# An unread full-array product in the empty places of attention's first steps

## The chip, the cores and the metric

The kernel runs on one NeuronCore of a Trainium2 chip. The metric is the device time of one execution in microseconds (us). Engine names are those of the profile: PE is TensorE's matmul, PEld its weight load, DVE is VectorE, ACT is ScalarE, POOL is GpSimd, SP is SyncE, which issues most DMAs. "Granted clock" (PEclk) is the share of TensorE's full clock that the throttle let through.

## What is computed

Two layers on 8 sequences of 512 tokens with 256 features, all in float32. Layer 0 is a bidirectional state-space mixer beside a mixture of eight experts that picks one expert per token. Layer 1 is attention with 16 heads of 16 features beside a mixture of seven experts (and a no-op), two per token, with a capacity per expert. Only layer 1 matters here:

```python
x = x + attention0(xn) + experts0(xn)
xn = layernorm(x)
scores = clip(q @ k.T * scale, -10000, 10000) * decay      # 16 heads, 512 x 512
scores = clip(scores)                                     # per batch
attn = softmax(scores); out = attn @ v                    # latent keys and values
x = x + out @ Wo + experts1(xn)                           # top 2 of 8, capacity 512 rows each
```

## The kernel before, in words

The program is one hand-ordered stream (each engine runs its instructions in the order in which the Python code issues them; a semaphore wait holds back everything behind it on the same engine). After the state-space layer comes attention, which is 128 **steps**: 8 batches, 4 groups of 4 heads, 4 tiles of 128 query rows. The loop `for n in range(N + 3)` (L1612) issues in each turn, in this order on PE:

- `scores` of step n (L1463): four products of 16x128 by 16x512, side by side in the array, each into one of the four `s_ps` banks. DVE then clips them (L1468) and multiplies by the decay band with a running maximum (L1470), four each; ACT takes the exponentials (L1478) one turn later.
- in even turns, `values` (L1494) of the two steps before: 16 products with 256 columns into `o_ps`.
- a place for other work, `fill()` (L1568).
- `transpose` (L1485) of heads 0 and 1 of step n-2: eight 128x128 transposes into the two `p_ps` banks, copied out by ACT (L1486).
- a second place, then the transposes of heads 2 and 3, then a third and a fourth place. So a turn of this part of the program has four places.

What goes into a place is decided by `fill()`: first a piece already begun (`half_done`), then `urgent` (the closing projections of a batch, `finish`, L1426), then `idle`, which is the second layer's experts, paced by `due()`. While the layer before still has rows to finish (`late_left`), it does one piece of those (`last_rows`). Otherwise the place stays empty and `fill()` returns false.

The experts can't begin at once. First the routing must be worked out (`route1`, L1189: some 50 DVE instructions, two products L201 and L202 and one exponential, issued by `follow()` at the end of each turn, two pieces a turn). Then `send_rows` (L1333) sends 32 tiles of 128 rows to their slots, two tiles a turn: per tile, one DVE copy of slots (L1365), one DVE product (L1353) and two indirect DMAs by POOL (L1346). The turn in which these run out is `ready`; it is n = 23. The expert pieces are offered from n = `ready` + 3 = 26 on (L1634). So in turns 5 to 25 the four places are empty, except for turn 23, where `finish` of batch 0 takes all four.

All filled-in work shares one PSUM buffer: `bank(name, shape)` (L1183) takes a tile with the tag `bank` and one buffer, so a product in it must wait until whoever read the bank's former content has done so. The expert pieces are each four matmul instructions of 128x128 by 256 columns (L1279 for the first matrix, L1292 for the second). A float32 product is two matmul instructions in the trace. `ident` is the 128x128 identity, and `band` the decay table, 128 x 896, both constants by that time.

Of the kernel before, what the change touches and what calls it, by code (L numbers as in the profile page):

```python
# [17 lines left out]
P = 128  # L18
B, S, DM = 8, 512, 256
# [40 lines left out]
def tile_kernel(ctx: ExitStack, tc: tile.TileContext, t, out: bass.AP):  # L60
    nc = tc.nc
    V, A, G, T, Y = nc.vector, nc.scalar, nc.gpsimd, nc.tensor, nc.sync
# [4 lines left out]
    def ctile(name, shape, dtype=FP, pool=None):  # L67
        return (pool or const).tile(shape, dtype, name=name, tag=name)
# [7 lines left out]
    ident = ctile("ident", [P, P])  # L76
# [281 lines left out]
    def bank(name, shape, tag="gen"):  # L358
        return mp.tile(shape, FP, name=name, tag=("e", "s")[tag] if isinstance(tag, int) else tag, bufs=2)
# [150 lines left out]
    with ExitStack() as es:  # L510
# [560 lines left out]
        with tc.manual_schedule(engines=ENGINES):  # L1071
# [34 lines left out]
            def fill(n):  # L1106
                for _ in range(n):
                    if next(rows, "end") == "end":
                        next(rest, None)

            for n in range(N):
# [16 lines left out]
                if n % 8 == 5 and next_:  # L1128
                    pending.append(beginning)
                fill(1)  # L1130
                if ahead:
                    ahead.cross(range(NH // 2))
                now.inside()
                if ahead:
                    ahead.cross(range(NH // 2, NH))
                turn()
                fill(1)
                now.before()
                if ahead:
                    ahead.pairs(batch[ahead.b])  # L1140
                fill(1)
                turn()
                now.behind()
# [35 lines left out]
    with tc.tile_pool(name="a1", bufs=1) as p1, tc.tile_pool(name="a2", bufs=2) as p2, tc.tile_pool(  # L1179
# [153 lines left out]
        def send_rows():  # L1333

            sent = []
            for i in range(NTILE):
                b, c = i // TPB, i % TPB
                if c == 0 and b + 2 < B:
                    ask_rows(b + 2)
                if c == 0:  # L1340
                    V.tensor_copy(to_send[b][:, :, DM : DM + NE], to_send["shares"][:, i : i + TPB, :])
                    V.tensor_copy(to_send[b][:, :, DM + NE :], bc(iota_n[:, i : i + TPB], 2, [P, TPB, NE]))
                x = to_send[b][:, c, :]
                at = turn(r1b, i)
                for k in range(2):
                    one = G.indirect_dma_start(  # L1346
                        out=xd1, out_offset=bass.IndirectOffsetOnAxis(ap=at[:, k : k + 1], axis=0),
                        in_=x, in_offset=None, bounds_check=NSLOT1 - 1, oob_is_err=False,
                    )
                    for other in sent:  # L1350
                        tc.declare_no_dep(one.ins, other.ins, reason="rows go to slots of their own")
                    sent.append(one)
                V.tensor_scalar(x_sb[:, i, :], x[:, :DM], noop[:, i : i + 1], None, ALU.mult)  # L1353
                yield
# [79 lines left out]
        def combine():  # L1434


            def add(b):
                G.dma_start(out=x_sb[:, b * TPB : (b + 1) * TPB, :], in_=rows_of(x1, b), accum_op=ALU.add)

            for b in (B - 1, *range(B - 2)):  # L1440
                add(b)
            yield
            while B - 2 not in finished:
                yield
            add(B - 2)
            for b in range(B - 1):
                G.dma_start(out=rows_of(out, b), in_=x_sb[:, b * TPB : (b + 1) * TPB, :])
# [92 lines left out]
        with tc.manual_schedule(engines=ENGINES):  # L1540
# [11 lines left out]
            def due():  # L1552

                return WORK * (n - ready - 2) / (LAST - ready - 2)

            rows, routing, sends, work, ready, e1 = combine(), route1(), send_rows(), None, None, None
# [4 lines left out]
            def last_rows(k):  # L1561

                nonlocal late_left
                for _ in range(k):
                    if next(rest, "end") == "end":
                        late_left = False

            def fill():  # L1568

                nonlocal spent  # L1570
                while queue := half_done or urgent or (idle if idle and spent < due() else []):
                    try:
                        spent += queue[0] is work
                        if next(queue[0]):
                            half_done[:] = queue[:1]
                        else:
                            half_done.clear()
                        return True
                    except StopIteration:
                        queue.pop(0)  # L1580
                if late_left:
                    last_rows(1)
                return late_left

            def more():
# [177 lines left out]
```

## Time and profile before

| | |
|---|---|
| median of 9 runs | 2038.75 us (2034.35 to 2045.25) |
| the profiled execution | 2037.76 us, of which its span (first to last instruction) is 2036.1 us |
| mean granted clock in it | 0.941 |
| PE busy | 1823.4 us, 90% of the span |
| DVE busy | 1450.4 us, 71% |
| ACT busy | 1150.8 us, 57% |
| POOL busy | 628.3 us, 31% |
| attention's first scores | 1132.60 us from the span's start |
| scores of turn 5 / 9 / 23 / 24 / 26 / 27 begin | 1183.10 / 1221.94 / 1307.68 / 1315.96 / 1326.88 / 1336.42 us |
| granted clock from 1342.5 to 1980 us | 1.00 |

A view of stretches ("windows") gives, for each stretch of the span, how long each engine was busy in it, with the number of instructions in brackets, and then PEclk, the DMA engines' share and GB/s. A timeline row gives the start, the time, the engine, the line, the operation, what is written and read, how many were merged into the row (x8), and in brackets the engine's idle time before it and what ended that. Matmuls are pipelined: the time of one contains its way through the array, so what a group of them costs PE is read from the start of the next group, not from the sum of durations.

### The profile page before, as it was taken

Reading aid. Unit: us, or ns where it says so; the run is one execution under the profiler, and the core shown is the slowest. Engines: PE = TensorE matmul, PEld = TensorE weight load, DVE = VectorE, ACT = ScalarE, POOL = GpSimd, SP = SyncE. Lnnn points to the kernel's source line nnn. Section 1 sums busy time; section 2 is a strip of 40 time slices with the busy share of each in tenths; the row PEclk is TensorE's granted clock in tenths of the full one; section 3 lists DMA queues with packets and bytes.
Section 4 is the critical chain, followed back from the end, with each engine's and each line's share of the span. In section 5 each row is a group of like instructions: output and inputs, shape, how many; then the busy total and the mean of one; then the engine's idle time right before and its main releaser. Section 6 shows DMA issues by size and latency. Waiting matters only on the chain.

```text
span 2036.1 us, 33675 instructions
## 1 busy us (share of the span) xinstructions
PE 1823.4 (90%) x11760; PEld 1226.4 (60%) x11760; DVE 1450.4 (71%) x3431; ACT 1150.8 (57%) x2511; POOL 628.3 (31%) x570
## 2 busy tenths in 40 slices
PE   5676899999999999998799578899999999999997
PEld 4433577676767777764455344566666666666654
DVE  5775666667576665769743579978787878787785
ACT  1143353535445353544443258778887887788876
POOL 0038644646355454634341006500000100000030
PEclk9876999999999999998798678899999999999998
DMA  7112565655556565634443334223132222313180
GB/s 268 62 42 97 194 215 165 215 169 189 169 156 218 175 199 177 197 110 140 150 161 111 110 100 147 67 69 96 44 99 52 75 78 56 100 35 105 35 166 11
DMA packets 152025, 255.68 MB, mean 126 GB/s; under 512 B 22537, under 2 KB 111484, under 8 KB 139952
## 3 DMA queue, kind: packets, MB, share of 16 engines
q1 hardware_dynamic: 113872, 132.94, 21.2%
q0 software_dynamic: 28512, 110.92, 17.8%
q10 hardware_dynamic: 9472, 9.67, 1.4%
q8 instruction: 94, 1.54, 0.3%
q14 instruction: 75, 0.61, 0.1%
HBM read 185.38 MB, written 73.07 MB: 127 GB/s over the span
## 4 chain that ended last, share of the span: by engine, by line
PE 64%; DVE 11%; ACT 9%; issue 2%; DMA 2%; POOL 1%; SPq 1%; ACTq 0%; DVEq 0%; POOLq 0%
PE p_ps L1485 8%; PE o_ps L1494 6%; PE h_ps L564 6%; PE y_ps L582 6%; PE pj L772 6%; PE s_ps L1463 5%; ACT s L1478 5%; PE e_yp L1292 5%; PE e_hp L1279 5%; ACT pT L1486 3%; PE op L914 2%; PE yd L994 2%; PE seg L956 2%; PE sp L1020 2%; PE yoff L1012 1%
## 5 line engine op out<-in xcount | busy, mean ns | idle before, releaser
L1468 DVE TENSOR_SCALAR s<-s_ps 128x512 f32<-128x512 f32 x512 | 317.8, 682 | 142.7 <-PE s_ps L1463 138.2
L1478 ACT ACTIVATE s<-s,ng 128x512 f32<-128x512 f32 x512 | 330.7, 716 | 0.0
L1486 ACT COPY pT<-p_ps 128x512 f32<-128x512 f32 x512 | 276.0, 588 | 86.5 <-PE p_ps L1485 79.9
L1470 DVE CUSTOM_DVE_ANT_0 s<-s,band 128x512 f32<-128x512 f32 x512 | 323.1, 685 | 0.0
L1485 PE MATMUL p_ps<-ident,s 128*128 128x128 f32 x2048 | 288.3, 284 | 29.5 <-ACT pT L1486 23.8
L1485 PEld LDWEIGHTS p_ps<-ident,s 128*128 128x128 f32 x2048 | 235.5, 144 | 112.1 <-ACT s L1478 41.0
L1298 POOL DMA_INDIRECT x<-e_yo,e_to x28 | 45.8, 1636 | 588.5 <-ACT e_yo L1297 351.9
L772 PE MATMUL pj<-xT,w_in 128*128 128x512 f32 x384 | 203.7, 657 | 12.6 <-DVE cv L785 7.8
L1463 PE MATMUL s_ps<-kT,qT 16*128 16x512 f32 x1024 | 169.3, 682 | 29.9 <-DVE s L1468 22.8
L564 PEld LDWEIGHTS h_ps<-xdT,w 128*128 128x128 f32 x1248 | 149.4, 193 | 22.6 <-issue 21.5
L564 PE MATMUL h_ps<-xdT,w 128*128 128x128 f32 x1248 | 153.0, 276 | 3.1 <-DMA w<-in_w_dram,w_idx 3.1
L785 DVE SCALAR_TENSOR_TENSOR cv<-pj,w_conv_w,cv 128x511 f32<-128x511 f32 (+2 forms) x192 | 143.1, 746 | 11.1 <-ACT cv L781 7.1
L582 PE MATMUL y_ps<-w,hT 128*128 128x256 f32 x624 | 149.7, 384 | 0.0
L940 POOL TENSOR_TENSOR au<-da,half 128x512 f32<-128x512 f32 x64 | 77.7, 1214 | 226.3 <-PE seg L956 125.5
L1494 PE MATMUL o_ps<-pT,vt 128*32 128x256 f32 x2048 | 138.2, 413 | 0.1
L582 PEld LDWEIGHTS y_ps<-w,hT 128*128 128x128 f32 x624 | 117.4, 193 | 32.7 <-issue 17.4
L772 PEld LDWEIGHTS pj<-xT,w_in 128*128 128x128 f32 x384 | 71.9, 205 | 96.4 <-issue 85.6
L1279 PE MATMUL e_hp<-e_xdT,e_w 128*128 128x256 f32 x448 | 120.7, 392 | 7.6 <-ACT e_hT L1282 6.8
L1014 POOL TENSOR_TENSOR yT<-yT,ex 128x512 f32<-128x512 f32 (+1 forms) x48 | 58.6, 1220 | 223.2 <-DVE ex L1013 157.8
L1494 PEld LDWEIGHTS o_ps<-pT,vt 128*32 128x32 f32 x2048 | 64.2, 117 | 95.2 <-issue 65.6
L1292 PE MATMUL e_yp<-e_w,e_hT 128*128 128x256 f32 x448 | 113.1, 385 | 0.5 <-ACT e_hT L1282 0.5
L994 PE MATMUL yd<-mt,xdt 128*64 128x128 f32 x1024 | 77.4, 298 | 38.8 <-DVE mt L988 38.8
(289 smaller groups left out, 3015.1 us busy)
## 6 DMA issues: line engine op xcount, KB each, us to landing
ex<-exd SPq DMA_DIRECT2D x96, 128.0 KB
u<-in_u_dram SPq DMA_DIRECT2D x16, 512.0 KB
fr<-fdd SPq DMA_DIRECT2D x64, 128.0 KB
od<-os SPq DMA_DIRECT2D x28, 256.0 KB
e_w<-in_ei_dram SPq DMA_DIRECT2D x7, 1024.0 KB
e_w<-in_eo_dram SPq DMA_DIRECT2D x7, 1024.0 KB
xd<-xd SPq DMA_DIRECT2D x39, 128.0 KB
yd<-yo SPq DMA_DIRECT2D x39, 128.0 KB
```

The lines of the kernel that those rows point to most:

```text
L564: T.matmul(hp[:, i, :], w1[:, k * FF + f * P : k * FF + (f + 1) * P], xdT[:, k * P : (k + 1) * P], start=(k == 0), stop=(k == KC - 1),)
L582: T.matmul(yp, hT[f // 4][:, f % 4, :], w2[:, f * DM : (f + 1) * DM], start=(f == 0), stop=(f == FC - 1))
L772: T.matmul(pj, w_in[:, k, o * P : (o + 1) * P], self.xT[:, k, :], start=(k == 0), stop=(k == KC - 1))
L1279: T.matmul(hp, w1[:, k, f * P : (f + 1) * P], xdT[:, k, :], start=(k == 0), stop=(k == KC - 1))
L1292: T.matmul(yp, hT[:, f, c * P : (c + 1) * P], w2[:, f, :], start=(f == 0), stop=(f == FC - 1))
L1463: T.matmul(sp[i], self.q[r, cols], self.k[r, :], start=True, stop=True)
L1468: V.tensor_scalar(self.p[i], sp[i], -CLAMP, CLAMP, ALU.max, ALU.min)
L1470: V.tensor_tensor_reduce(out=self.p[i], in0=self.p[i], in1=band[:, at : at + S], scale=1.0, scalar=-3.0e38, op0=ALU.mult, op1=ALU.max, acc ...
L1478: A.activation(self.p[i], self.p[i], AF.Exp, bias=self.ng[:, i : i + 1])
L1485: T.transpose(pp[:, k, :], self.p[i][:, k * P : (k + 1) * P], ident)
L1486: A.copy(pT[i][:, :, cc * P : (cc + 1) * P], pp)
L1494: T.matmul(op[32 * i : 32 * i + 32, half * 2 * P : (half + 1) * 2 * P], self.v[:, k, h * (AD + 1) : h * (AD + 1) + 32], pT[i][:, k, :], st ...
```

## The change

Where `fill()` finds nothing, and the experts are not yet offered, it issues one product of the identity with the first 512 columns of the decay band, into the shared bank. Nobody reads it. `fill()` goes on returning `late_left`, which is false there, so what its callers do after it is as before.

```diff
@@ fill()
                 if late_left:
                     last_rows(1)
+                elif ready is None or n < ready + 3:
+                    T.matmul(bank("warm", [P, S]), ident, band[:, :S], start=True, stop=True)
                 return late_left
```

On PE the new order has 80 of these products (160 matmul instructions): four in each of turns 5 to 22, 24 and 25, none elsewhere. In a turn they stand after `scores` (and `values`), between the two pairs of transposes, and two behind the second pair. The order of the other engines' instructions and of all DMAs is as before.

## The prediction

> **What bounds the kernel now.** I read the page's slices first, to see where PE's clock drops; then the stretches of the turns concerned; then the timeline of PE inside a turn, to see what a filled place costs. The slices, each 50.9 us long (first rows of the page):
>
> ```profile
> PE   5676899999999999998799578899999999999997
> ...
> DVE  5775666667576665769743579978787878787785
> ...
> PEclk9876999999999999998798678899999999999998
> ```
>
> Attention begins in the 23rd slice (1132.60 us). From there to the 27th PE's digit is low, and so is its clock; afterwards both stand at 9. The change aims at turns 5 to 25. The stretches: turns 5 to 8, turns 9 to 22, a later pair of turns (49 and 50) in which all four places hold expert pieces, and the expert stretch.
>
> ```profile
> 1183.10:1221.94 38.84, 27.22 (x165) 14.70 (x164) 34.46 (x100) 19.22 (x35) 2.67 (x4) 0.78 0.35 105
> 1221.94:1307.68 85.74, 74.62 (x561) 41.18 (x560) 85.22 (x267) 66.64 (x117) 56.61 (x58) 0.86 0.32 100
> ...
> 1483.62:1498.43 14.81, 14.81 (x114) 10.78 (x113) 10.19 (x26) 11.34 (x21) 1.55 (x1) 1.00 0.42 129
> ...
> 1342.50:1980.00 637.50, 611.60 (x4845) 415.94 (x4845) 510.30 (x1340) 512.59 (x959) 61.49 (x43) 1.00 0.29 75
> ```
>
> The third number of busy time is DVE's. In turns 9 to 22 DVE is busy for 85.22 of 85.74 us, though PE's clock is only 0.86: **DVE sets the pace there**, at 85.74/14 = 6.12 us a turn; its first clips of neighbouring turns start 5.9 to 6.0 us apart (1242.49, 1248.45, 1254.38 us in its timeline), filled with four clips, four band products and two tiles of the sends. In turns 5 to 8 the DVE chain of the routing is without a gap from 1186.69 us, when the exponential it waits for arrives, to 1219.06 us, and PE waits for it:
>
> ```profile
> 1212.24 3.86 PE L1463 MATMUL s_ps<-kT,qT 16*128 16x512 f32 x8 [6.35 <-DVE s L1468]
> ```
>
> So PE is slow here because it waits; little waits for PE.
>
> **What one filled place costs.** The trace has no product nobody reads, but it has full-array float32 products of the same shape (L253, 128x128 by 512 columns; four instructions are two products), at full clock:
>
> ```profile
> 1168.74 1.96 PE L253 MATMUL qp<-xT,w_w_q 128*128 128x512 f32 x4
> ...
> 1170.54 1.04 PE L1485 MATMUL p_ps<-ident,s 128*128 128x128 f32 x8
> ```
>
> Two products hold PE for 1170.54 - 1168.74 = 1.80 us, 0.90 us each. An expert piece is the same amount (four instructions of half the columns), and it stands in just the places the change fills. Turn 49, an odd one, with four pieces:
>
> ```profile
> 1483.62 1.14 PE L1463 MATMUL s_ps<-kT,qT 16*128 16x512 f32 x8
> 1484.69 1.13 PE L1292 MATMUL e_yp<-e_w,e_hT 128*128 128x256 f32 x4
> 1485.66 1.04 PE L1485 MATMUL p_ps<-ident,s 128*128 128x128 f32 x8
> 1486.53 1.03 PE L1292 MATMUL e_yp<-e_w,e_hT 128*128 128x256 f32 x4
> 1487.40 1.04 PE L1485 MATMUL p_ps<-ident,s 128*128 128x128 f32 x8
> 1488.27 1.89 PE L1292 MATMUL e_yp<-e_w,e_hT 128*128 128x256 f32 x8
> 1490.09 1.14 PE L1463 MATMUL s_ps<-kT,qT 16*128 16x512 f32 x8
> ...
> 1498.43 0.71 PE L1463 MATMUL s_ps<-kT,qT 16*128 16x512 f32 x4
> ```
>
> From start to start: scores 1.07, piece 0.97, transposes 0.87, piece 0.87, transposes 0.87, two pieces 1.82, together 6.47 us, without idle time. The even turn 50 has the values as well and takes 1498.43 - 1490.09 = 8.34 us. A pair is 14.81 us, of PE alone, at full clock.
>
> **The change part by part.**
>
> *Turns 9 to 22* (14 turns, four products each). PE needs 7 x 6.47 + 7 x 8.34 = 103.7 us, DVE still 85. PE becomes the bound: 103.7 - 85.7 = **+17.9 us**. I take the pair's 14.81 us whole: the pieces and the new products are the same stream of columns. Two ends: a product that waits for nothing may let PE load weights earlier. The least is the streaming alone: a single piece costs 0.87 us where it is hemmed in, the first 0.97, so at most 0.1 us a turn goes, -1.4 us. Upward, half-clock time in these turns now costs (see the rivals).
>
> *Turns 24 and 25*: now 10.92 us, then 14.81: **+3.9 us**. Turn 23 keeps its 8.28 us, its places being taken by `finish`.
>
> *Turn 26* now takes 9.54 us at a granted clock of 0.73 with PE busy throughout, so 0.27 x 9.54 = 2.6 us are clock. If PE has been dense before, as it is from 1342.5 us on with a clock of 1.00: **-2.6 us**. Nothing if the clock stays down.
>
> *Turns 5 to 8* (16 products, 14.4 us). PE has room: 38.84 us of wall against 2 x 14.81 = 29.6 us. Their cover is the DVE chain. Turn 5: last transposes at 1187.18, done by 1188.3; two products more, 1190.1; next scores wait for DVE until 1190.90. Turn 6: the routing's products L201 and L202 move behind two more products, but DVE reads them only at 1204.86 (L204), behind its clips. Turn 7 has the one **new wait**: its first product takes the bank that L204 must have read, 1204.86 + 0.68 = 1205.54 us. Behind it on PE stand the turn's transposes and scores of turn 8, behind those ACT's copies and exponentials. PE is done 0.97 + 0.87 + 0.87 + 0.87 + 1.82 = 5.40 us later, at 1210.94, and scores of turn 8 can't start before 1212.24. In turn 8 the cover ends: at full clock scores (gated by the clips until 1213.9), values 1.87 and 5.40 of the rest end near 1221.7, against 1221.94 now; at half clock, as now until about 1219, near 1224.9. I take 0, and keep -0.3 and +3.0.
>
> *The rest.* Turn 24's first product waits for the copy of the last `finish` piece, covered by scores and values (1.07 + 1.87 us). DVE, ACT, POOL and the DMA queues get no instruction, and no issue moves in its queue. From turn 26 on PE is busy for 611.60 of 637.50 us; the pace of the expert pieces goes by the turn's number, so a delay isn't caught up: it moves the end.
>
> Sum: 17.9 + 3.9 - 2.6 + 0 = **+19.2 us**. The profiled execution, 2037.76 us, becomes 2057.0. It lies 1.0 us below the median of the runs shown, so I predict **2058 us**.
>
> **Rules of the skill.** The row gives 0.90 us for a product of 512 columns in float32. The Trainium skill, "TensorE: Matmul & The Clock Gate", section "Back-to-back issue gap", puts the gap of an N = 512 matmul at about 216 ns, without naming a type; by it a turn would gain only 0.86 us of PE work, all hidden below DVE, and the sum would be about the same or a small gain. The trace decides: two instructions a product, 0.45 us each. The same page ("Why this matters for your kernels") asks for no PE gaps over about 3 us; the trace has a 6.35 us gap in turn 7 and a clock of 0.78 around it, which agrees, but it says nothing of who waits for that clock.
>
> **The rivals.**
>
> *Faster: the clock was the bound, and the products fit.* Clock lost between 1183.10 and 1336.42 us: 38.84 x 0.22 + 85.74 x 0.14 + 10.92 x 0.08 + 9.54 x 0.27 = 24.0 us; that is the ceiling, 2014 us in the profile's terms. For it: the chain of waits in this stretch goes through PE's o_ps, p_ps and s_ps for 46% and DVE's two lines for 9%. Against: DVE is 85.22 of 85.74 busy, and at its 5.9 us a turn little more than 14 x 0.2 + 2.6 + 0.9 = 6.3 us can come back: 2032 us. The decisive price: a pair without pieces is 14.81 - 8 x 0.87 = 7.9 us, DVE's pair 11.8, so a product must cost under 3.9/8 = 0.49 us. The rows say 0.87 to 0.90.
>
> *Same: the products land in gaps that stay gaps,* as in turns 5 to 8, or PE already had such room: 74.62 of 85.74 us busy at 0.86 clock. 2039 us, at most 2043. Against: four products are 3.5 us a turn, the room of the rival above is 3.9/2 = 1.95 us.
>
> *Slower than forecast: the clock goes on dipping.* PE being the bound, each lost share counts in full. At the present 0.86 over 118 us of dense turns: 118 x 0.14/0.86 = 19 us more, and no -2.6: 2080. At 0.95, 6 us more: 2064. For it: the clock drops here now. Against: steps packed like this run at 1.00 for 637 us.
>
> **How the numbers follow.** The forecast and its ends (2053 to 2064) get 0.80, dipping beyond that 0.12, same 0.05, faster 0.03. The range is 2049 to 2069: the known ends, -1.7 and +3, some dips, and 4 us on each side for the spread of the runs. 0.3% is about 6 us, what a measurement of this kernel can tell from no change.
>
> **What would show it.** In the changed profile: turns 9 to 22 about 104 us long with PE as good as without idle and PEclk near 1.00; pairs of 14.8 us; DVE idle there for some 18 us, waiting for PE's s_ps; scores of turn 9 at 1222 as before, and of turn 27 at 1356. Wrong, if a product costs under 0.8 us between its neighbours, if PEclk stays at 0.86, or if turns 5 to 8 grow by more than 3 us.

## The result, and the profile after

The changed kernel takes 2057.22 us (median of 19 runs, 2048.31 to 2066.45), the kernel before 2037.03 us (62 runs on the same chips): a ratio of 1.0100, 95% interval 1.0087 to 1.0114, which is 20.2 us more. The forecast was 2058 us. Its profiled execution took 2063.84 us, 6.6 us above its median, so the table below, which is made from profiles, is to be read for where the time lies and not for the total.

| us | turns 5-8 | 9-22 | 23 | 24-25 | 26 | sum of 5-26 |
|---|---|---|---|---|---|---|
| before | 38.8 | 85.7 | 8.3 | 10.9 | 9.5 | 153.3 |
| forecast | 38.8 | 103.7 | 8.3 | 14.8 | 7.0 | 172.6 |
| after | 42.1 | 107.9 | 8.3 | 15.4 | 7.1 | 180.9 |

The stretches of the changed kernel, one for each column of the table. Columns: the stretch, its length, then busy time and instructions of PE, PEld, DVE, ACT and POOL, the granted clock, the DMA share and GB/s.

```profile
1185.62:1227.73 42.11, 40.49 (x197) 18.96 (x196) 36.89 (x110) 21.21 (x39) 4.16 (x5) 0.88 0.32 101
1227.73:1335.68 107.95, 107.14 (x673) 53.03 (x673) 84.36 (x261) 66.78 (x117) 57.50 (x58) 1.00 0.25 78
1335.68:1343.94 8.26, 6.74 (x41) 4.84 (x41) 6.18 (x16) 5.58 (x11) 2.93 (x3) 1.00 0.27 86
1343.94:1359.36 15.42, 15.30 (x97) 7.58 (x97) 10.62 (x27) 9.76 (x19) 0.00 (x0) 1.00 0.38 118
1359.36:1366.47 7.11, 7.11 (x69) 4.80 (x68) 5.55 (x16) 4.75 (x9) 0.00 (x0) 1.00 0.38 109
```

In the second row the clock is 1.00 and PE is busy for 107.14 of 107.95 us. DVE has nearly the same work as before (84.36 us) and now stands idle for the other 23.6: the bound has gone from DVE to PE. Turn 26 runs at full clock (7.11 us, forecast 6.96); whether the new products are the reason comes below.

The same in the slices and groups of the changed kernel's page, where a slice is 51.6 us long. The last row is DVE's clip: its own line, busy time and mean ns of one, then the idle time before it and what ended most of that.

```profile
PEclk9877999999999999998798699999999999999998
...
L1468 DVE TENSOR_SCALAR s<-s_ps 128x512 f32<-128x512 f32 x512 | 317.8, 683 | 168.5 <-PE s_ps L1463 164.0
```

In the slices 24 to 26, where before had 788 for the clock, it now has 999 (PE's own digits went from 788 to 999 as well); the clip waits 25.8 us longer for PE's scores than before (138.2 us there).

Two adjoining turns, 17 and 18, in PE's timeline of the changed kernel (start, time, engine, line, operation):

```profile
1289.42 1.14 PE L1463 MATMUL s_ps<-kT,qT 16*128 16x512 f32 x8
1290.49 1.12 PE L1584 MATMUL warm<-band,ident 128*128 128x512 f32 x2
1291.45 1.04 PE L1485 MATMUL p_ps<-ident,s 128*128 128x128 f32 x8
1292.32 1.02 PE L1584 MATMUL warm<-band,ident 128*128 128x512 f32 x2
1293.18 1.04 PE L1485 MATMUL p_ps<-ident,s 128*128 128x128 f32 x8
1294.06 2.21 PE L1584 MATMUL warm<-band,ident 128*128 128x512 f32 x4
1296.19 1.14 PE L1463 MATMUL s_ps<-kT,qT 16*128 16x512 f32 x8
...
1304.84 0.71 PE L1463 MATMUL s_ps<-kT,qT 16*128 16x512 f32 x4
```

From start to start this is 1.07, 0.96, 0.87, 0.86, 0.88 and 2.13 us: every step as forecast, except for the last two products together, 2.13 instead of 1.82. The turns take 6.77 and 8.65 us instead of 6.47 and 8.34. The weight loads beside the last row show why:

```profile
1293.95 0.30 PEld L1584 LDWEIGHTS warm<-band,ident 128*128 128x128 f32 x2
1295.14 0.30 PEld L1584 LDWEIGHTS warm<-band,ident 128*128 128x128 f32 x2 [0.89 <-PE warm L1584]
```

The fourth product's loads come 1.19 us after the third's, and the release is PE itself, at the end of the third product. Each call of `bank` makes a new tile in the one buffer, so the fourth product waits on PE's semaphore for the third to have left the array. In turns 5 to 26 the trace has 20 such waits, 17.7 us of idle time at PEld; 0.31 us of each reaches PE. My forecast said that such a product "waits for nothing".

In turns 5 to 8, PE was at half clock in turn 6, as before, but now with more to do. From PE's timeline there:

```profile
1193.42 3.86 PE L1463 MATMUL s_ps<-kT,qT 16*128 16x512 f32 x8 [0.53 <-DVE s L1468]
1197.21 3.64 PE L1494 MATMUL o_ps<-pT,vt 128*32 128x256 f32 x32
1200.78 1.62 PE L1584 MATMUL warm<-band,ident 128*128 128x512 f32 x2
...
1204.84 2.21 PE L1584 MATMUL warm<-band,ident 128*128 128x512 f32 x4
1207.11 0.70 PE L201 MATMUL both<-mask,row_lt 128*128 128x256 f32 x2
```

and from DVE's:

```profile
1208.28 0.69 DVE L204 COPY rk_b<-both 128x512 f32<-128x512 f32 x1 [0.80 <-PE both L202]
```

Scores and values take 3.79 and 3.57 us from start to start, where a turn at full clock needs 1.07 and 1.87. The routing's products L201 and L202 follow the four new ones, and for once DVE waits for them, 0.80 us. The forecast had them ready before DVE came; that failed with the clock down (a run below has the same products here at a better clock, without this wait). Turn 6 takes 14.75 us instead of 11.38, turn 7 7.51 instead of 9.96. Turn 8 takes 12.1 us instead of 9.7, partly at half clock still, with a wait of 0.66 us for a DMA of `kT`. Together that is +3.3 us.

### The profile page after: what moved, and what is told of

It is laid out like the page before. It is cut to its first block, busy times and chain, and to the rows that moved or that the text cites. A ratio compares the mean times of both kernels' runs of the same rounds, so it can differ in the third digit from the quotient of the medians.

```text
span 2062.1 us, 33955 instructions
## 1 busy us (share of the span) xinstructions
PE 1867.4 (91%) x11920; PEld 1242.8 (60%) x11920; DVE 1450.9 (70%) x3431; ACT 1151.3 (56%) x2511; POOL 629.5 (31%) x570
## 4 chain that ended last, share of the span: by engine, by line
PE 67%; DVE 10%; ACT 7%; issue 2%; DMA 2%; POOL 1%; SPq 1%; ACTq 0%; DVEq 0%; POOLq 0%
PE p_ps L1485 9%; PE y_ps L582 6%; PE h_ps L564 6%; PE o_ps L1494 6%; PE pj L772 6%; PE s_ps L1463 5%; PE e_yp L1292 5%; PE e_hp L1279 4%; ACT s L1478 4%; PE warm L1584 3%; PE op L914 2%; PE yd L994 2%; PE seg L956 2%; ACT pT L1486 2%; PE sp L1020 2%
## 5 line engine op out<-in xcount | busy, mean ns | idle before, releaser
L1485 PE MATMUL p_ps<-ident,s 128*128 128x128 f32 x2048 | 279.7, 279 | 15.0 <-ACT pT L1486 11.3
L1463 PE MATMUL s_ps<-kT,qT 16*128 16x512 f32 x1024 | 159.1, 657 | 21.8 <-DVE s L1468 14.0
L785 DVE SCALAR_TENSOR_TENSOR cv<-pj,w_conv_w,cv 128x511 f32<-128x511 f32 (+2 forms) x192 | 143.0, 745 | 10.9 <-ACT cv L781 6.9
L1494 PE MATMUL o_ps<-pT,vt 128*32 128x256 f32 x2048 | 130.5, 396 | 0.0
```

The costliest lines, as they stand in the source:

```text
L1463: T.matmul(sp[i], self.q[r, cols], self.k[r, :], start=True, stop=True)
L1485: T.transpose(pp[:, k, :], self.p[i][:, k * P : (k + 1) * P], ident)
L1494: T.matmul(op[32 * i : 32 * i + 32, half * 2 * P : (half + 1) * 2 * P], self.v[:, k, h * (AD + 1) : h * (AD + 1) + 32], pT[i][:, k, :], st ...
```

## The experiments

The theory, as after the result: PE's own stream sets turns 9 to 22, because DVE's pace leaves room for only about two of the products a turn. The main rival: each product costs the turn its length from the first one on (linear). Another: clock and dense issue, not PE time, decide. Every kernel was timed against the kernel before on its own chip; the kernel before itself was profiled once more.

### How many and how large: four kernels

The first has 128 columns instead of 512 in each product:

```diff
-                    T.matmul(bank("warm", [P, S]), ident, band[:, :S], start=True, stop=True)
+                    T.matmul(bank("warm", [P, P]), ident, band[:, :P], start=True, stop=True)
```

> The 80 products keep their places, but have 128 columns, a quarter. Theory (a turn is as long as the longer of PE's stream and DVE's 5.9 us): a product streams 0.21 us in place of 0.85, so a pair of turns needs about 15.4 - 8 x 0.64 = 10.3 us of PE, below DVE's 11.8. Turns 9 to 22 stay at 85 to 86 us as before the change, whatever the clock; only turns 24 to 26 can gain up to 3.5 us from a better clock. Time 2033 to 2038, a ratio of 0.998 to 1.0005 to the kernel before. Rival (the clock was the bound, and only the long products are in the way): the small products keep the clock up and turns 9 to 22 become clearly shorter than 85 us, 10 us or more in all: under 2027.

The second fills only the first two places of a turn, the third the first three (`<= 3`):

```diff
+                    warmed.append(n)
+                    if warmed.count(n) <= 2:
                         T.matmul(bank("warm", [P, S]), ident, band[:, :S], start=True, stop=True)
```

> Only the first two places of a turn get the full product (40 products). Theory (room): a pair of turns takes 14.81 - 2 x 1.82 = 11.2 us of PE at full clock, just under DVE's 11.8, so turns 9 to 22 stay at 84 to 87 us; time within 4 us of before, 2034 to 2041. Rival (each product costs its 0.9 us wherever it stands): half of the 80 products, half of the loss, +10 us: 2047.

> The first three places get the full product (60 products). Theory (room): odd turn 1.07 + 0.97 + 0.87 + 0.87 + 0.87 + 0.91 = 5.56, even turn 7.43, a pair 13.0 against DVE's 11.8: turns 9 to 22 about 91 us, 24 and 25 about 13, turn 26 about 7; with two or three us for turns 5 to 8, about +7 to +10 us: 2044 to 2047. Rival (each product costs the same wherever it stands): three quarters of the loss, +15: 2052. No two products stand back to back here, so the wait of one product for the other doesn't enter.

The fourth has all four products, but one tile a turn, so that no product waits for the one before it:

```diff
-                    T.matmul(bank("warm", [P, S]), ident, band[:, :S], start=True, stop=True)
+                    if not warmed or warmed[0] != n:
+                        warmed[:] = [n, bank("warm", [P, S])]
+                    T.matmul(warmed[1], ident, band[:, :S], start=True, stop=True)
```

> The same 80 full products, but those of one turn write one and the same tile, so that a product doesn't wait for the one before it to have left the array. Theory (the 0.31 us a turn over the forecast are that wait, between the third and the fourth place): turns take 6.47 and 8.34 us in place of 6.78 and 8.64, turns 9 to 22 103.7 us in place of 107.9, some 6 us in all: 2051. Rival (the product is simply longer than an expert piece of the same amount): turns stay at 6.78 and 8.64, 2057.

Turns 9 to 22 of the four kernels, in the order quarter, two, three, one tile (columns as in the first table of stretches):

```profile
1223.69:1305.86 82.17, 78.42 (x674) 51.94 (x673) 81.69 (x254) 66.16 (x117) 54.84 (x56) 1.00 0.34 104
```

```profile
1225.89:1307.74 81.85, 81.85 (x617) 45.67 (x616) 81.37 (x254) 65.90 (x117) 54.54 (x56) 1.00 0.34 103
```

```profile
1221.92:1313.30 91.38, 91.38 (x645) 48.86 (x645) 83.63 (x259) 66.80 (x117) 55.66 (x56) 1.00 0.31 92
```

```profile
1221.92:1325.32 103.40, 103.40 (x674) 54.19 (x673) 84.68 (x263) 66.79 (x117) 59.73 (x57) 1.00 0.26 81
```

With none, two, three and four products a turn (the last with one tile) these turns take 85.7, 81.9, 91.4 and 103.4 us. That is a kink and not a line: two products cost nothing here, and the third and the fourth 9.5 and 12.0 us. The ratios to the kernel before agree: 0.9977 [0.9951, 1.0004] with quarters, 0.9976 [0.9957, 0.9995] with two, 1.0037 [1.0016, 1.0059] with three and 1.0092 [1.0063, 1.0122] with one tile. The linear rival falls, since two products would have given 10 us more.

The first two kernels came out below the 84 to 87 us that I expected. But a turn is counted here from PE's scores to its next scores, and PE can run ahead of DVE. DVE's own timeline gives DVE's pace. These are the first clips of turns 9 and 23, in the kernel before and then in the one with two products:

```profile
1224.90 2.47 DVE L1468 TENSOR_SCALAR s<-s_ps 128x512 f32<-128x512 f32 x4
...
1308.91 2.48 DVE L1468 TENSOR_SCALAR s<-s_ps 128x512 f32<-128x512 f32 x4 [0.55 <-PE s_ps L1463]
```

```profile
1227.58 2.47 DVE L1468 TENSOR_SCALAR s<-s_ps 128x512 f32<-128x512 f32 x4
...
1310.94 2.47 DVE L1468 TENSOR_SCALAR s<-s_ps 128x512 f32<-128x512 f32 x4
```

They are 84.01 and 83.36 us apart, and 83.36 again with the quarters. So DVE went only 0.65 us faster. Most of the 3.6 to 3.9 us by which these turns are shorter is PE's lead: before, DVE came 2.96 us behind PE's scores in turn 9 and 1.23 us in turn 23; with two products 1.69 and 3.20 us. Turn 23 takes the lead back: there PE waits for DVE (`oT`) and ACT (`fo`), and the turn lasts 10.5 us with two products and 10.2 with quarters instead of 8.3. Turns 9 to 23 together take 94.0 us before, 92.4 with quarters and 92.4 with two products.

Read by pairs of turns, then, the bound is the larger of two sums: DVE's 11.9 us (83.36/7) and PE's 7.9 + 0.87 per product, which is 11.4 for four products, 13.1 for six (measured 91.38/7 = 13.05) and 14.9 for eight (measured 14.77).

The same two kernels say what the clock is worth by itself in this place. Both have it at 1.00, where before had 0.86, and both gain 1.7 us in turns 9 to 23: DVE is busy for all but 0.5 us, and hardly goes faster. With products of 128 columns the forecast's first rival comes true in its mechanism, since they cost less than its decisive price of 0.49 us; but the 6 us that the forecast allowed it was nearer than the 24 us of lost clock. In turns 24 and 25 two products did cost time: 14.4 us instead of 10.9, at a granted clock of 0.78, after PE had waited 2.36 us for ACT at the end of turn 23.

Four products on one tile give back 107.95 - 103.40 = 4.55 us of these turns, and turns of 6.45 and 8.32 us, from its PE timeline, the last row being the one to compare with the 2.13 us above:

```profile
1281.00 1.14 PE L1463 MATMUL s_ps<-kT,qT 16*128 16x512 f32 x8
...
1285.64 1.88 PE L1587 MATMUL warm<-band,ident 128*128 128x512 f32 x4
1287.46 1.14 PE L1463 MATMUL s_ps<-kT,qT 16*128 16x512 f32 x8
...
1295.77 0.71 PE L1463 MATMUL s_ps<-kT,qT 16*128 16x512 f32 x4
```

So the wait of a product for its predecessor is shown as the cause of the 0.31 us: taken away with nothing else changed, the two products take 1287.46 - 1285.64 = 1.82 us, and the turns have the length that the forecast gave them. The medians can't tell this kernel from the changed one (1.0092 [1.0063, 1.0122] against 1.0100 [1.0087, 1.0114]); the turns can.

### Which turns: four runs on another chip

The next set was to tell the parts of the change by place: products in turns 5 to 8 alone (first diff), two a turn from turn 9 on (second), and the latter with 14 products more in turn 1, before the loads there. The fourth run is the kernel before, profiled on the same chip.

```diff
+                elif n < 9:
+                    T.matmul(bank("warm", [P, S]), ident, band[:, :S], start=True, stop=True)
```

```diff
+                elif n >= 9 and (ready is None or n < ready + 3):
+                    warmed.append(n)
+                    if warmed.count(n) <= 2:
+                        T.matmul(bank("warm", [P, S]), ident, band[:, :S], start=True, stop=True)
```

```diff
+                if n == 1:
+                    before_it = bank("warm", [P, S])
+                    for _ in range(14):
+                        T.matmul(before_it, ident, band[:, :S], start=True, stop=True)
```

> The four full products stand only in turns 5 to 8 (16 of the 80). Theory (DVE's routing chain covers them, what they cost is only the half clock that is granted there): turns 5 to 8 take 40 to 42 us against 38.8 in the profile of before, turns 9 to 22 85 to 86 as before; time +1 to +3.5 us, 2038 to 2042. Rival (each product costs its price wherever it stands): 16 x 0.9 = +14 us, 2052.

> Two full products a turn, in the first two places, from turn 9 on only. Theory: turns 5 to 8 return to 38.8 to 39.5 us, turns 9 to 22 stay at 82 at a clock of 1.00 (PE 11.2 us a pair, DVE 11.7), turn 26 at 7.1: 1 us below the kernel with two products from turn 5 on, some 7 us below the kernel before: 2028 to 2034. Rival (the products of turns 5 to 8 are what brings the clock up for turn 9): half clock comes back in turns 9 and 10, and the time is no better than with two products from turn 5 on.

> As the kernel with two products from turn 9 on, and 14 more full products in turn 1, where PE waits 13.9 us for DVE and the clock stands at half. Theory (there PE's chain sets the time of turns 2 to 4, and the clock goes up after some us of dense products): scores of turn 2 start when they did, within 1 us, then run at full clock; turn 2 takes 8 us in place of 11.6, the rest as before; 3 to 4 us below the kernel with two products from turn 9 on. Rival (turns 2 to 4 wait for DVE and DMA, not for the clock): no gain, or a loss of up to 3 us where the products are still running at half clock when turn 2's scores could start.

> The kernel before, once more, for a second profile of it. Theory: turns 9 to 22 at 84 to 88 us with some half-clock time in them again, turns 24 to 26 at 18 to 21 us. If turns 9 to 22 stand under 83 us or show no half clock, the first profile was no fair base for the sum.

On this chip the kernel before takes 2056.9 us (median of 29 runs), 20 us more than on the others, so the absolute expectations could not be tested. The ratios are 1.0023 [0.9997, 1.0048] for turns 5 to 8 alone, 0.9999 [0.9979, 1.0020] for two from turn 9, and 0.9986 [0.9963, 1.0009] with the products in turn 1: none is told from no change. The first interval ends at +10 us, so the rival of +14 us for turns 5 to 8 falls. Here is the stretch of turns 9 to 22 of the kernel before on this chip:

```profile
1225.30:1334.63 109.33, 83.40 (x562) 47.34 (x561) 86.18 (x267) 68.14 (x117) 58.52 (x60) 0.72 0.25 78
```

109.33 us instead of 85.7, with DVE busy for hardly longer. In these turns PE and ACT stand idle together, in all four kernels of this chip, for up to 6 us at a time and at uneven distances. In the kernel before PE has seven idle times over 1.5 us here, 19.5 us together; in the first profile of that kernel it has none. An example is the one with two products from turn 9, ACT's timeline and then PE's:

```profile
1238.37 0.58 ACT L1512 COPY os<-o_ps 128x512 f32<-128x512 f32 x1 [5.82 <-remote]
```

```profile
1238.43 2.08 PE L1587 MATMUL warm<-band,ident 128*128 128x512 f32 x2 [4.44 <-remote]
```

"remote" means that the profile names no instruction of the core as the releaser. Other stops are put down to PE and ACT waiting for each other, or to nothing. The instruction loads and DMAs around the stops show no difference to the other chips; the cause stays open.

What can be kept of this set: products in turns 5 to 8 alone raised the clock of those turns from 0.74 to 0.96 and left their length as it was (39.25 and 39.58 us). So there the cover of DVE's chain held. Turn 6 took 11.6 us in this run, and L202 was ready for DVE; in turn 7 PE waited 1.96 us for L204 instead, the new wait that the forecast had named, and the four turns grew no longer by it. The same products in the changed kernel took 42.1 us with turn 6 at half clock, which points to the clock of turn 6 as what decides their cost.

With the 14 products in turn 1, turn 2 took 10.2 us instead of 12.3, and turns 1, 3 and 4 were 1.0, 1.9 and 1.6 us longer. Turns 3 and 4 together vary from 18.1 to 21.4 us between profiles without these products, so one profile of each kernel doesn't show what the products did there.

### The changed kernel and two products again, and a lighter DVE

The changed kernel and the one with two products were run once more, on a third chip, where the kernel before takes 2035.21 us. Beside them, one kernel without any new product tested the theory from DVE's side: the product of each tile that is sent (one of DVE's two instructions there) goes to ACT, which was busy for 66.64 of 85.74 us in turns 9 to 22.

```diff
-                V.tensor_scalar(x_sb[:, i, :], x[:, :DM], noop[:, i : i + 1], None, ALU.mult)
+                A.mul(x_sb[:, i, :], x[:, :DM], noop[:, i : i + 1])
```

The last kernel has both: this edit, and two products of 256 columns in each turn from turn 9 on.

```diff
+                elif n >= 9 and (ready is None or n < ready + 3):
+                    warmed.append(n)
+                    if warmed.count(n) <= 2:
+                        T.matmul(bank("warm", [P, HS]), ident, band[:, :HS], start=True, stop=True)
```

> The changed kernel once more. Theory: turns 9 to 22 at 107.9 us (6.78 and 8.64 a turn) wherever PE isn't stopped by something else, since they are PE's stream alone; ratio 1.008 to 1.012. If this core shows the stops of 4 us that the second profile of before had in turns 9 to 22, they add to these turns as they do to those of before: again about 1.01. Rival (there the stops leave the clock low, and the products repair that): ratio under 1.005 in such a place.

> Two full products a turn, once more, on the core that runs the changed kernel. Theory: turns 9 to 22 at 82 us, ratio 0.996 to 0.999 where PE isn't stopped; the difference to the changed kernel 20 us or more.

> The kernel before, with no added products, but the two products L1353 of each turn of the sends done by ScalarE in place of VectorE. Theory (DVE sets the pace of turns 9 to 22): DVE loses about 0.55 us of its 5.9 a turn, ACT has 66.6 of 85.7 us busy and takes 0.8 more; turns 9 to 22 fall to 78 to 82 us, 4 to 8 us in all. Rival (PE's chain with its low clock sets the pace): turns 9 to 22 stay at 85 to 86 us.

> L1353 on ScalarE, and two products of 256 columns a turn from turn 9 on. Theory: PE needs 7.9 + 4 x 0.45 = 9.7 us a pair, DVE 10.6, at a full clock; turns 9 to 22 at 75 to 78 us, turn 26 at 7.1; 10 to 13 us below the kernel before: ratio 0.994 to 0.995. Rival (products add nothing to what the lighter DVE gives): the same as the run with ScalarE alone.

The changed kernel is slower again, 1.0078 [1.0055, 1.0101], with turns of the same length (6.78 and 8.64 us, 107.96 us for turns 9 to 22). Two products a turn again gain a little: 0.9976 [0.9956, 0.9997], after 0.9976 in the first set, with 81.66 us for turns 9 to 22 and 91.9 for turns 9 to 23.

DVE's lighter load by itself brought nothing: 1.0000 [0.9981, 1.0019], and its turns 9 to 22 missed the forecast of 78 to 82 us widely. Its stretches of all these turns, and of turns 15 to 17, then the one with both edits:

```profile
1220.24:1313.10 92.86, 75.84 (x562) 41.19 (x561) 77.34 (x235) 77.47 (x145) 59.14 (x58) 0.80 0.29 92
1261.86:1278.59 16.73, 12.06 (x106) 6.92 (x105) 15.88 (x46) 15.89 (x31) 10.81 (x11) 1.00 0.30 99
```

```profile
1219.81:1303.96 84.15, 74.29 (x618) 44.48 (x617) 77.25 (x232) 76.17 (x145) 58.63 (x58) 0.96 0.32 101
```

DVE's work fell from 85.2 to 77.3 us, and where the clock stayed up, the turns did get shorter: 16.73/3 = 5.58 us each. But the clock was at 0.80 on the whole, and five of the seven pairs of turns took 13.7 to 14.0 us, each with a dip in it, against 11.1 for the pair without. So "DVE alone sets the pace" was too simple: with its load taken down, DVE waits 14.9 us for PE's scores in these turns, and PE sets the pace wherever its clock is down. The edit also put work on ACT, and PE's wait for ACT's copies of `pT` in each odd turn rose from 1.04 to 1.83 us. Whether these longer waits bring on the dips, no run here tells apart.

With two half-width products a turn the clock is 0.96, and the same turns take 84.15 us instead of 92.86. I expected 75 to 78. Two dips remain, which cost 1.5 us each (pairs of 13.1 us instead of 11.6). The rest goes with PE's wait for ACT's copies in each odd turn, which the forecast left out:

```profile
1224.33 1.14 PE L1485 MATMUL p_ps<-ident,s 128*128 128x128 f32 x8 [1.40 <-ACT pT L1486]
```

Seven such waits make 9.8 us; even without the dips the turns would take 7 x 11.6 = 81 us.

The time is 2025.49 us (median of 6), 0.9930 [0.9907, 0.9954], the best of this study. The profiles explain only a small part of that: turns 9 to 23 take 92.9 us here, no less than with two full products alone (91.9), and turns 5 to 26 are 3.8 us shorter than in the kernel before, against 14 us by the ratio. The half-width products from turn 9 on were not run without the other edit, so that both are needed together is plausible and not shown.

## Why the prediction was right

**The price of a product and the change of the bound** held. The expert pieces in the same places were the right model: 6.47 and 8.34 us forecast, 6.45 and 8.32 measured where the products don't wait for each other. DVE's idle time, the clock of 1.00 and turn 23 (8.28 forecast, 8.26 measured) came as forecast. Two readings were a little off: the low digits of the slices end with the 26th and not the 27th, and DVE's own pace before was 84.01/14 = 6.00 us a turn, since the 85.7 us contain 1.7 us of PE's lead that shrinks.

**Turn 26: the right length, and not for the reason given.** The forecast took 2.6 us off because dense products would bring the clock up. The turn did take 7.11 us. But it took 7.11 us as well in three profiles that have no new product in turns 9 to 25: the kernel before on the second chip, the one with products in turns 5 to 8, and the one with L1353 on ACT. So the 9.54 us belong to the one profile of before from which the forecast was made, and the change can't be credited with the difference.

**Mis-sized: "a product that waits for nothing".** I counted waits on other engines and forgot the bank's own former content when nobody reads it. The two expert pieces that I took as the model accumulate into one tile; each of the new products asks for a tile of its own. It costs 0.31 us a turn, 4.3 of the 22.2 us in turns 9 to 22 and 0.6 in turns 24 and 25.

**Mis-sized: turns 5 to 8,** taken as 0 with an upper end of +3.0, measured +3.3, so one of the forecast's own signs of being wrong (a growth of more than 3 us) came true. The end that the forecast worked out for half clock in turn 8 was the right one; that the clock would also delay L202 past DVE's copy wasn't in it, though turn 6 already ran its scores and values at half clock before (7.4 us). Scores of turn 9 came at 1227.7 and of turn 27 at 1366.5 us, forecast 1222 and 1356; 2.5 us of that arose before turn 5.

**Right in part by compensation.** In the profiles turns 5 to 26 grew by 27.5 us, 8.3 more than the forecast's 19.2, but the medians differ by 20.2 only. The same gap shows in the other kernels on the two ordinary chips. The turns' difference from before's one profile stands beside the measured ratio, converted to microseconds (the change's by its medians, the others by the ratio less 1 times the median of before on that chip):

| kernel | turns 5-26 by profile | by the ratio |
|---|---|---|
| four products (the change) | +27.5 | +20.2 |
| the same, third chip | +27.7 | +15.9 |
| four, one tile | +21.1 | +18.8 |
| three | +7.6 | +7.5 |
| two | +0.6 | -4.9 |
| two, third chip | +0.6 | -4.9 |
| four quarters | -2.8 | -4.7 |
| product on ACT | +4.4 | 0.0 |
| product on ACT, two halves | -3.8 | -14.2 |

The second number is always the lower one, by 0.1 to 11.8 us. A before that mostly spends some 5 us more in these turns than in the execution that was profiled would give this, and its clock dips there do come and go; turn 26 speaks for the opposite. There is one profile of before on such a chip, and an unprofiled run can't be split; the closing turns 118 to 125 also differ from profile to profile, 52.5 us in before and one of the two-product runs, 46.9 to 49.8 in the others. How the 7 us divide stays open. That the median came within 1 us of the forecast is therefore in part luck: the terms it had too small, 8 us together, were made up for by something that no run here shows.

**The rivals.** The first, faster, fell where the forecast put it: a product costs 0.86 to 0.87 us, over 0.49 (the first of a turn 0.96). "Same" fell with it, and continued dips didn't come from turn 9 on (clock 1.00).

## What to carry to other kernels

Before filling the idle places of an engine, take the pace of the engine that sets the turn, and subtract the stream that the idle one already has; here the room was 11.8 - 7.9 = 3.9 us a pair, so that two products of 0.87 us a turn cost nothing in turns 9 to 23, and eight a pair, 7 us, overran it by some 3 us. A raised clock is worth only what waits for that engine: 1.7 to 2.1 us here in turns 9 to 23, out of 12 us of lost clock, and in turns 9 to 22 four products of 128 columns a turn held it as well as two of 512. Where the bound was taken off the other engine, a dip of the clock did lengthen the turns. And compare engines by their own timelines: a stretch cut at one engine's instructions also contains what that engine gains or loses of its lead.

## What the runs showed of the hardware

- In this program a product into a new tile of a single PSUM buffer waits until PE's former product into it has left the array, even when nobody reads it: the weight load stood idle for 0.89 us, and two products took 2.13 instead of 1.82 us.
- In turns 9 to 22 of the kernel before the longest idle time of PE that its waits show is 1.0 us (for ACT's copies of `pT`), and yet the granted clock was 0.86. The Trainium skill, "TensorE: Matmul & The Clock Gate", section "Why this matters for your kernels", asks for no gaps over about 3 us. By the trace, idle times shorter than that don't ensure the full clock. But from the end of an odd turn's scores to the next scores PE does nothing besides waiting except transposes (3.7 us in turn 9), and no run here tells whether those count for the clock. Products of 128 columns in four places of each turn brought it to 1.00.
- One of the chips ran the same kernel 20 us longer; in turns 9 to 22 PE and ACT stood idle together there, and for several of these idle times, the 5.82 us of ACT above among them, the profile names no instruction of the core as the cause.
